# Next tokens of a fused attention and FFN kernel: transposes on TensorE, or in 32x32 squares on VectorE with DMAs that place the squares

## The chip, the cores and the metric

The kernel runs on one core of one Trainium2 chip. The metric is the device time of one execution in microseconds (us); lower is better. A core has five engines that run programs of their own: TensorE (PE in the profile), VectorE (DVE), ScalarE (ACT), GpSimd (POOL) and SyncE (SP), which here issues nearly all DMAs.

## The reference

Eight sequences of 512 tokens with 512 features, in fp32. Each is normalised, goes through a linear attention and through a gated FFN with Hadamard transforms, and the two results are multiplied and added to the input:

```python
xn = _layernorm(x, axis=-1)
q, k, v = xn @ Wq.T + bq, xn @ Wk.T + bk, xn @ Wv.T + bv          # 512 -> 512
kv_sum = cumsum((elu(k) + 1) * v, axis=tokens)
s = ((elu(q) + 1) * kv_sum * SCALE) @ Wo.T + bo
h = fwht(xn * SU_ug) / 64                                          # Hadamard over 512
h = silu(h @ W_gate.T * (wg * 64)) * (h @ W_up.T * (wu * 64))      # 512 -> 2048
g = silu((fwht(h * SU_dp) / 64) @ W_down.T * (Wscale_dp * 64))     # 2048 -> 512
out = x + s * g
```

## The kernel before

*Pairs and factors.* The eight sequences are taken in four pairs `p`, two sequences `s` at a time. All large products are done by a Strassen-like scheme: a 2x2 block product in seven products instead of eight, with sums and differences of blocks before and after. The seven factors of an operand are called `P1, P2, P7, P3, P4, P5, P6` (places 0 to 6). The operand with the tokens is `xo`, a tile of 128 x 7 x 7 x 256: 128 features on the partitions, 7 outer factors, 7 inner factors, 256 tokens. The outer 2x2 blocks are sequence by half of the features: P1 and P2 are the two halves of the first sequence's features, P3 and (for a while) P7 those of the second's; P5, P6, P4 and the final P7 are differences of these. The inner blocks are half of the tokens by tile of 128 features, places 0 to 3; the other three are differences. `group` uses outer factors alone, `block_product` both.

*Getting the tokens.* `load_x` (L105) loads a sequence with tokens on the partitions, `layernorm` (L116) normalises it on VectorE, with one square root on ScalarE. `transposed` (L137) then brings features onto the partitions: for each of four token tiles, four TensorE transposes into one PSUM tile `pt` (L142). For the first sequence of a pair ScalarE copies `pt` into the outer factors P1 and P2 (L146); for the second, ScalarE copies one half (L149) and VectorE forms P5, P6 and P7 with one operand from PSUM (L150 to L152), and at last P4 (L155). At the start of a later pair `inner_tokens` (L157) forms the inner factors P5, P6 and P4 for all seven outer factors. `xo` is allocated anew for each pair in a pool with one buffer.

*A pair.* `attention` makes the key, value and query products (`group`, L306) and the scan over the tokens; `project_out` the output product, kept in DRAM as `d_s`. Then four hidden units `u` follow: in the first pair `gate` and `up` on folded weights, which also make the weights of later pairs and store them in DRAM (`inner_w`, whose sums `s_gate` and `s_up` take the one buffer of the pool `xin`, as `load_x` does for later sequences); in later pairs `hidden_unit` (L647), which calls `block_product` (L467) for seven outer factors in the order P1, P5, P6, P2, P7, P3, P4. After two units `down` does half of the last product, after four the other half, with the gating of the output:

```python
steps += [(p2, 0), (p6, 0), (p2, 1), (p6, 1)]
steps += [(p, g) for p in (p5, p3, p4) for g in range(2)]
```

`token_groups` (L376) runs it: first `p1` and `p7` for two halves `g` of the tokens, then the steps above. Three kinds of PSUM bank are used: `px` (three buffers), `py` (one) and `pz` (two). `p2` multiplies into `py` and VectorE empties it with `output` (L406); so `p2(1)` can start only when the output of `p2(0)` is done. `read` (L402) takes an intermediate sum out of `px` (`sa_dn`, `sb_dn`, `sc_dn`). Each factor `i` has a weight tile, loaded by `get_w` in the order P1, P7, P2, P6, P5, P3, P4: `w_down_0`, `w_down_2`, `w_down_1`, `w_down_6`, `w_down_5`, `w_down_3`, `w_down_4` (the number is the place). The second `down` of a pair also needs the kept sums `d` (twice) and `s` (twice), fetched from DRAM, and the inputs `y` (twice), loaded again, 1 MB each; `gated` applies SiLU on ScalarE (L710), multiplies on POOL (L712), and adds on VectorE (L713).

*What sets the order.* The Python code uses a small agenda (`at`, `advance`) to interleave steps of neighbouring products. After that a scheduler gives each engine its program: it takes instructions by priority (order in the code; `background()` puts a piece 150 places back) as their operands are expected to be ready. The resulting program of each engine is fixed when the kernel is built. An engine carries it out in order, so an instruction that waits for a semaphore holds all that stands behind it on that engine; for SP this is true of the DMAs it issues. A tile in a pool with one buffer can be filled again only when all readers of its last content are done.

Of the kernel before, what the change touches and what calls it, by code (L numbers as in the profile page):

```python
# [8 lines left out]
F32 = mybir.dt.float32  # L9
AF = mybir.ActivationFunctionType  # L10
ALU = mybir.AluOpType
# [6 lines left out]
P1, P2, P7, P3, P4, P5, P6 = range(7)  # L18
# [3 lines left out]
def kernel(  # L22
# [27 lines left out]
    nc = tc.nc  # L50
    P = 128
    B, L, D = x.shape
    FF = wup_t.shape[1]
    KD = D // P
# [4 lines left out]
    H = L // 2  # L59
# [4 lines left out]
    xop = ctx.enter_context(tc.tile_pool(name="xop", bufs=1))  # L64
    hop = ctx.enter_context(tc.tile_pool(name="hop", bufs=2))
    wpool = ctx.enter_context(tc.tile_pool(name="wpool", bufs=4))
    xin = ctx.enter_context(tc.tile_pool(name="xin", bufs=1))
# [4 lines left out]
    dram = ctx.enter_context(tc.tile_pool(name="dram", bufs=1, space=DRAM))  # L72

    @contextmanager
    def background(behind=150):

        at = tc.cur_priority
        tc.cur_priority = at + behind
        yield
        tc.cur_priority = at  # L80
# [4 lines left out]
    at = 0  # L85
# [19 lines left out]
    def load_x(b, t=None, parts=1):  # L105
        if t is None:
            t = xin.tile([P, 3, 7, P], F32, tag="x", name=f"x_{b}")
            t = t.rearrange("p c s e -> p (c s e)")[:, : NT * D].rearrange("p (n d) -> p n d", n=NT)
        n = NT // parts
        for i in range(0, NT, n):  # L110
            nc.sync.dma_start(
                t[:, i : i + n], x[b, i * P : (i + n) * P, :].rearrange("(n p) d -> p n d", p=P)
            )
        return t

    def layernorm(b, xt, parts=1):  # L116
        n = NT // parts
        for i in range(0, NT, n):
            mv = small.tile([P, n, 2], F32, tag="mv", name=f"mv_{b}_{i}")
            for t in range(n):  # L120
                st = small.tile([P, 6], F32, tag="st", name=f"st_{b}_{i}_{t}")
                nc.vector.bn_stats(st, xt[:, i + t, :])
                nc.vector.bn_aggr(mv[:, t, :], st)
            rstd = small.tile([P, n], F32, tag="rstd", name=f"rstd_{b}_{i}")
            nc.vector.tensor_scalar(rstd, mv[:, :, 1], EPS, None, ALU.add)
            nc.scalar.activation(rstd, rstd, AF.Sqrt)
            nc.vector.reciprocal(rstd, rstd)
            for t in range(n):
                nc.vector.tensor_scalar(
                    xt[:, i + t, :], xt[:, i + t, :], mv[:, t, 0:1], rstd[:, t : t + 1],  # L130
                    ALU.subtract, ALU.mult,
                )

    def transposed(b, xt, xo):  # L137
        s = b % 2
        for t in range(NT):
            pt = ps.tile([P, KD, P], F32, tag="t", name=f"pt_{b}_{t}")  # L140
            for c in range(KD):
                nc.tensor.transpose(pt[:, c, :], xt[:, t, c * P : (c + 1) * P], ident)  # L142
            q = 2 * (t // 2)
            o = xo[:, :, q : q + 2, t % 2 * P : t % 2 * P + P]
            if s == 0:
                nc.scalar.copy(o[:, P1 : P2 + 1], pt.rearrange("p (h j) t -> p h j t", h=2))  # L146
            else:
                b12, b22 = pt[:, 0:2], pt[:, 2:4]
                nc.scalar.copy(o[:, P3], b22)  # L149
                nc.vector.tensor_tensor(o[:, P5], b12, o[:, P1], ALU.subtract)  # L150
                nc.vector.tensor_tensor(o[:, P6], b22, o[:, P5], ALU.subtract)
                nc.vector.tensor_tensor(o[:, P7], o[:, P3], b12, ALU.subtract)  # L152
        if s == 1:
            o = xo[:, :, 0:4]
            nc.vector.tensor_tensor(o[:, P4], o[:, P2], o[:, P6], ALU.subtract)  # L155

    def inner_tokens(xo):  # L157

        nc.vector.tensor_tensor(xo[:, :, P5], xo[:, :, P7], xo[:, :, P1], ALU.subtract)
        nc.vector.tensor_tensor(xo[:, :, P6], xo[:, :, P3], xo[:, :, P5], ALU.subtract)  # L160
        nc.vector.tensor_tensor(xo[:, :, P4], xo[:, :, P2], xo[:, :, P6], ALU.subtract)

    def inner_t3(xo, factors):
        for i in factors:
            nc.vector.tensor_tensor(xo[:, i, P7], xo[:, i, P3], xo[:, i, P7], ALU.subtract)
# [17 lines left out]
    kept = {}  # L183
# [102 lines left out]
    def at(place, fn):  # L286
        agenda.append((now[0] + place, now[1], fn))
        now[1] += 1
# [10 lines left out]
    def drain():  # L299
        advance(max([0] + [e[0] + 1 - now[0] for e in agenda]))  # L300
# [572 lines left out]
    def get_w(m, g):  # L873
# [15 lines left out]
    xs = [  # L889
        load_x(b, hop.tile([P, 2, 7, D], F32, tag="h", name=f"x_{b}")[:, 0, :NT], parts=2)  # L890
        for b in range(2)
    ]
# [5 lines left out]
    for i in range(7):  # L898
        dst = had if i % 2 == 0 else had2
        s = src.rearrange("p (a t h) -> p a t h", t=2, h=1 << i)  # L900
        d = dst.rearrange("p (a t h) -> p a t h", t=2, h=1 << i)
# [3 lines left out]
    xo = xop.tile([P, 7, 7, H], F32, tag="xo", name="xo_0")  # L905
# [29 lines left out]
    for p in range(B // 2):  # L935
        if p:
            with background():
                inner_tokens(xo)
        co = attention(p, xo, get_w)
        if p:  # L940
            inner_t3(xo, (P1, P5, P6, P2, P7))
            at(9, lambda: inner_t3(xo, (P3, P4)))
        more = p + 1 < B // 2
        hos = []

        def next_x():
            xs = [load_x(2 * p + 2), load_x(2 * p + 3)]
            for s in range(2):
                layernorm(2 * p + 2 + s, xs[s])
            return xs  # L950

        for u in range(NU):
            if p == 0:
                gs = [gate(p, u, xo, get_w)]
                gs.append(gate(p, u + NU, xo, get_w))
                if u == 0:
                    project_out(p, co, get_w)
                ho = hop.tile([P, 2, 7, L], F32, tag="h", name=f"ho_{p}_{u}")
                for m in range(2):
                    up(p, u + m * NU, gs[m], xo, ho[:, m], get_w)  # L960
            else:
                ho = hop.tile([P, 2, 7, L], F32, tag="h", name=f"ho_{p}_{u}")
                hidden_unit(p, u, xo, ho, get_w, u % 2 == 1)
                if u == 0:
                    project_out(p, co, get_w)
            hos.append(ho)
            if more and u == (2 if p else 3):
                xs = next_x()
            if u == 1:
                down(p, 0, hos, get_w)  # L970
                hos = []
        if more:
            xo = xop.tile([P, 7, 7, H], F32, tag="xo", name=f"xo_{p + 1}")
            for s in range(2):
                transposed(2 * p + 2 + s, xs[s], xo)
        ds, ss = [], []
        for s in range(2):
            ds.append(fetch(f"d_{p}_{s}"))
            ss.append(fetch(f"s_{p}_{s}"))
        ys = [load_y(p, s) for s in range(2)]  # L980
        down(p, 1, hos, get_w, ds, ss, ys)
        drain()
# [50 lines left out]
```

## Time and profile before

| what | value |
|---|---|
| time, median of three runs | 1605.21 us (1602.78 to 1605.37) |
| the profiled execution | 1606.13 us, span 1604.3 us from first to last instruction |
| PE busy | 1550.9 us, 97% |
| VectorE, ScalarE, POOL busy | 949.2, 425.1, 504.9 us |
| granted TensorE clock, mean | 0.992 |
| DMA | 254.29 MB, 47.9% of 16 engines' span on SP's queue |
| TensorE transposes (L142) | 128 |

The page of the profile gives busy times per engine, a chain of work that ended last (followed back from the last instruction to what released each step), and groups of instructions by source line with their mean duration and the idle time before them. A timeline lists one engine's instructions in order of time: start, duration, engine and line, operation, output and inputs, shape, count, and in brackets the idle time before it and who ended it. In this trace every fp32 matmul is recorded as two instructions: a `down` step of 8 matmuls appears as x16. Durations of neighbouring matmuls overlap, so what a stretch of PE costs is read from the starts.

### The profile page before, as it was taken

How to read it: one execution, taken by the hardware profiler on the slowest of the kernel's cores; microseconds unless marked ns; L12 is line 12 of the kernel's file. 1: busy time of each engine (PE TensorE's matmuls, PEld its weight loads, DVE VectorE, ACT ScalarE, POOL GpSimd, SP SyncE). 2: the span in 40 equal slices, each digit the busy share in tenths (PEclk: the TensorE clock that was granted, in tenths of full speed). 3: DMA queues.
4: the chain of work that ended last, by engine and by line, in shares of the span. 5: the costliest groups of instructions: out<-in, count | busy, mean ns of one | idle time of the engine just before them, and what ended most of it. 6: DMA issues, size and time to landing. Idle time of an engine off the chain costs nothing.

```text
span 1604.3 us, 15681 instructions
## 1 busy us (share of the span) xinstructions
PE 1550.9 (97%) x5936; PEld 1117.1 (70%) x5936; DVE 949.2 (59%) x1335; ACT 425.1 (26%) x679; POOL 504.9 (31%) x286
## 2 busy tenths in 40 slices
PE   6979989999999999999999999999999999999998
PEld 3335435854485478888886478888887468888887
DVE  6869666268565574715675475634675466542673
ACT  3333322132324431111222531111221441111211
POOL 4531342103322235302622236201622137120731
PEclk9999999999999999999999999999999999999999
DMA  8234559397763244335574232535474224525472
GB/s 266 80 111 135 180 148 300 84 280 215 250 218 129 69 138 145 131 107 189 178 255 144 90 107 102 193 91 188 158 265 157 69 93 137 176 83 190 141 261 84
DMA packets 147723, 254.29 MB, mean 159 GB/s; under 512 B 7232, under 2 KB 109120, under 8 KB 143552
## 3 DMA queue, kind: packets, MB, share of 16 engines
q1 hardware_dynamic: 147360, 253.00, 47.9%
q8 instruction: 47, 0.77, 0.2%
q10 hardware_dynamic: 288, 0.30, 0.1%
q14 instruction: 28, 0.23, 0.0%
HBM read 183.53 MB, written 69.73 MB: 158 GB/s over the span
## 4 chain that ended last, share of the span: by engine, by line
PE 73%; DVE 12%; DMA 5%; issue 4%; POOL 3%; ACT 2%; SPq 1%; POOLq 0%; DVEq 0%; ACTq 0%
PE px_gu L475 18%; PE pz_gu L475 9%; PE px_dn L391 8%; PE py_gu L475 5%; PE pz_dn L391 4%; PE px_o L391 3%; PE px_v L316 3%; PE px_k L316 3%; PE px_q L316 3%; PE py_dn L391 2%; DMA x<-in_x_dram 2%; POOL s L712 2%; PE pz_o L391 2%; PE pz_q L316 2%; PE pz_k L316 1%
## 5 line engine op out<-in xcount | busy, mean ns | idle before, releaser
L475 PE MATMUL px_gu<-xo,w_gu 128*128 128x256 f32 x1344 | 320.6, 380 | 0.0
L475 PEld LDWEIGHTS px_gu<-xo,w_gu 128*128 128x128 f32 x1344 | 254.7, 190 | 39.9 <-issue 3.6
L391 PE MATMUL px_dn<-w_down,ho 128*128 128x256 f32 x1024 | 230.1, 379 | 2.2 <-DVE sb_dn L402 1.7
L391 PEld LDWEIGHTS px_dn<-w_down,ho 128*128 128x128 f32 x1024 | 193.6, 190 | 31.4 <-DVE sb_dn L402 2.7
L475 PE MATMUL pz_gu<-xo,w_gu 128*128 128x256 f32 x672 | 173.1, 380 | 0.0
L675 POOL TENSOR_TENSOR u<-u,v 128x1024 f32<-128x1024 f32 x24 | 56.1, 2360 | 354.2 <-DVE u L513 354.2
L475 PEld LDWEIGHTS pz_gu<-xo,w_gu 128*128 128x128 f32 x672 | 127.0, 190 | 19.1 <-DVE a L517 0.9
L391 PE MATMUL pz_dn<-w_down,ho 128*128 128x256 f32 x512 | 116.6, 380 | 1.9 <-POOL ho L172 1.9
L391 PEld LDWEIGHTS pz_dn<-w_down,ho 128*128 128x128 f32 x512 | 96.4, 190 | 17.6 <-POOL ho L172 2.7
L712 POOL TENSOR_TENSOR s<-s,d 128x512 f32<-128x512 f32 x30 | 43.0, 1435 | 166.2 <-ACT d L710 166.2
L475 PE MATMUL py_gu<-xo,w_gu 128*128 128x256 f32 x336 | 86.2, 379 | 0.0
L563 POOL TENSOR_TENSOR v<-v,k 128x1024 f32<-128x1024 f32 x16 | 39.8, 2486 | 138.5 <-ACT v L538 110.3
L637 POOL TENSOR_TENSOR ho<-g,u 128x512 f32<-128x512 f32 x8 | 17.8, 2224 | 186.0 <-DVE u L332 186.0
L475 PEld LDWEIGHTS py_gu<-xo,w_gu 128*128 128x128 f32 x336 | 63.9, 190 | 8.7
L316 PE MATMUL px_k<-xo,w_k 128*128 128x512 f32 x128 | 63.0, 616 | 3.7 <-ACT sa_k L328 3.4
L316 PE MATMUL px_up<-xo,w_up 128*128 128x512 f32 x128 | 60.4, 600 | 4.0 <-DVE w_up L178 4.0
L679 POOL TENSOR_TENSOR v<-v,r 128x1024 f32<-128x1024 f32 x24 | 56.2, 2364 | 25.6 <-DVE r L513 25.6
L316 PE MATMUL px_v<-xo,w_v 128*128 128x512 f32 x128 | 60.2, 593 | 3.5 <-ACT sc_v L328 3.5
L316 PE MATMUL px_q<-xo,w_q 128*128 128x512 f32 x128 | 60.2, 593 | 0.0
L316 PE MATMUL px_gate<-xo,w_gate 128*128 128x512 f32 x128 | 59.6, 593 | 0.0
L565 DVE TENSOR_TENSOR_SCAN k<-ones,v 128x512 f32<-128x512 f32 x32 | 39.4, 1271 | 33.5 <-POOL v L563 33.5
L391 PE MATMUL py_dn<-w_down,ho 128*128 128x256 f32 x256 | 58.0, 379 | 0.0
(241 smaller groups left out, 2469.0 us busy)
## 6 DMA issues: line engine op xcount, KB each, us to landing
w_gu<-d_gu SPq DMA_DIRECT2D x84, 896.0 KB, 4.5
w_down<-d_down SPq DMA_DIRECT2D x56, 512.0 KB, 3.6
d_s<-o SPq DMA_DIRECT2D x8, 1024.0 KB, 4.4
d_d<-dn SPq DMA_DIRECT2D x8, 1024.0 KB, 7.5
d<-d_d SPq DMA_DIRECT2D x8, 1024.0 KB, 6.2
s<-d_s SPq DMA_DIRECT2D x8, 1024.0 KB, 7.3
y<-in_x_dram SPq DMA_DIRECT2D x8, 1024.0 KB, 8.4
out_dram<-y SPq DMA_DIRECT2D x16, 512.0 KB, 3.1
```

The costliest lines, as they stand in the source:

```text
L316: nc.tensor.matmul(p.rearrange("p a t -> p (a t)") if len(r.shape) == 2 else p, ws[k][:, i, :], r, start=(first and k == 0), stop=(k == n ...
L391: nc.tensor.matmul(p[:, c], t[:, (2 * g + c) * P : (2 * g + c + 1) * P], ws[i](k), start=(first and k == 0 and c == 0), stop=(k == n - 1), ...
L475: nc.tensor.matmul(p[:, lane], w[:, lane, i, :], x[:, i, :], start=(first and lane == 0), stop=True, skip_group_check=True,)
L563: nc.gpsimd.tensor_tensor(v[:, h], v[:, h], k[:, h], ALU.mult)
L565: nc.vector.tensor_tensor_scan(k[:, h, s], ones.to_broadcast([P, L]), v[:, h, s], 0.0, ALU.mult, ALU.add)
L637: nc.gpsimd.tensor_tensor(ho[:, P1], g[:, 0, 0], r[:, 0, 0], ALU.mult)
L675: nc.gpsimd.tensor_tensor(r[:, m], ru1[:, m], rv[:, m], ALU.add)
L679: nc.gpsimd.tensor_tensor(rv[:, m], rv[:, m], rr[:, m], ALU.add)
L712: (nc.vector if last else nc.gpsimd).tensor_tensor(r, r, d, ALU.mult)
```

## The change

The first pair is as before. For later pairs three new steps replace `next_x` and the TensorE transposes:

- `normalized(b)` loads and normalises a sequence and stores the result in DRAM as `d_x`. It is called after hidden units 0 and 1 of the pair before, in the background, instead of after unit 2 or 3.
- `squares(b)` loads the stored sequence back into a tile `z` in the pool `xin` with 16 DMAs. Each moves 32x32 squares: for a block `j` of 32 features within a feature tile `c`, the 32 tokens of each of the 16 token blocks go to the partitions `32 j` to `32 j + 31`. Every run is 32 features, 128 bytes.
- `turned(place, z, h, xo)` transposes the squares in place on VectorE, 32x32 at a time, straight into the outer factor `place` of `xo`: two instructions of 128x512 per factor.

`next_tokens` puts them together after the last hidden unit and ahead of the second `down`, with the differences P5, P6, P7 and P4 on VectorE from SBUF. `xo` is no longer allocated for each pair: one tile, made for the first pair, is written again for all.

```diff
+    def normalized(b):
+
+        xt = load_x(b)
+        layernorm(b, xt)
+        d = dram.tile([L, D], F32, tag=f"d_x_{b}", name=f"d_x_{b}")
+        nc.sync.dma_start(d.rearrange("(n p) d -> p n d", p=P), xt)
+        kept[f"x_{b}"] = d
+
+    def squares(b):
+
+
+        z = xin.tile([P, 3, 7, P], F32, tag="x", name=f"z_{b}")
+        z = z.rearrange("p c s e -> p (c s e)")[:, : KD * L].rearrange("p (c i f) -> p c i f", c=KD, f=32)
+        d = kept[f"x_{b}"].rearrange("(i t) (c j f) -> j t c i f", t=32, j=4, f=32)
+        for j in range(4):
+            for c in range(KD):
+                nc.sync.dma_start(z[32 * j : 32 * j + 32, c], d[j, :, c])
+        return z
+
+    def turned(place, z, h, xo):
+
+        for j in range(2):
+            nc.vector.transpose(
+                xo[:, place, j : j + 3 : 2, :], z[:, 2 * h + j].rearrange("p i f -> p (i f)")
+            )
+
+    def next_tokens(b, xo):
+
+        o = xo[:, :, 0:4]
+        z = squares(b)
+        turned(P1, z, 0, xo)
+        turned(P2, z, 1, xo)
+        z = squares(b + 1)
+        turned(P7, z, 0, xo)
+        nc.vector.tensor_tensor(o[:, P5], o[:, P7], o[:, P1], ALU.subtract)
+
+        def rest():
+            turned(P3, z, 1, xo)
+            nc.vector.tensor_tensor(o[:, P6], o[:, P3], o[:, P5], ALU.subtract)
+            nc.vector.tensor_tensor(o[:, P7], o[:, P3], o[:, P7], ALU.subtract)
+
+        def last():
+            nc.vector.tensor_tensor(o[:, P4], o[:, P2], o[:, P6], ALU.subtract)
+
+        at(5, rest)
+        at(10, last)
...
-        def next_x():
-            xs = [load_x(2 * p + 2), load_x(2 * p + 3)]
-            for s in range(2):
-                layernorm(2 * p + 2 + s, xs[s])
-            return xs
...
-            if more and u == (2 if p else 3):
-                xs = next_x()
+            if more and u < 2:
+                with background():
+                    normalized(2 * p + 2 + u)
             if u == 1:
                 down(p, 0, hos, get_w)
                 hos = []
         if more:
-            xo = xop.tile([P, 7, 7, H], F32, tag="xo", name=f"xo_{p + 1}")
-            for s in range(2):
-                transposed(2 * p + 2 + s, xs[s], xo)
+            next_tokens(2 * p + 2, xo)
```

## Prediction

> **What bounds the kernel now.** I read the page first, then the stretches of 25 us, then each engine's timeline around the three places where one pair of sequences hands over to the next. I call these seams: seam 1 lies at about 430 to 498 us, seam 2 at 800 to 869, seam 3 at 1169 to 1238. A seam holds the second `down` of a pair, the transposes of the next pair's tokens, and the next pair's first key product.
>
> ```profile
> PE 1550.9 (97%) x5936; PEld 1117.1 (70%) x5936; DVE 949.2 (59%) x1335; ACT 425.1 (26%) x679; POOL 504.9 (31%) x286
> PE 73%; DVE 12%; DMA 5%; issue 4%; POOL 3%; ACT 2%; SPq 1%; POOLq 0%; DVEq 0%; ACTq 0%
> ```
>
> TensorE (PE) is busy 97% of the span and carries 73% of the chain that ended last. From 300 us on, nearly every stretch of 25 us is full; what is missing lies at the seams. So only two things move the time: work taken off PE, and waits of PE. The PE timeline of seam 2 and then of seam 1 shows both:
>
> ```profile
> 807.88 1.04 PE L142 MATMUL pt<-ident,x 128*128 128x128 f32 x8
> 808.75 1.89 PE L391 MATMUL px_dn<-w_down,ho 128*128 128x256 f32 x8
> ...
> 826.49 3.62 PE L391 MATMUL py_dn<-w_down,ho 128*128 128x256 f32 x16
> ...
> 835.63 3.62 PE L391 MATMUL py_dn<-w_down,ho 128*128 128x256 f32 x16
> ...
> 868.93 1.98 PE L316 MATMUL px_k<-xo,w_k 128*128 128x512 f32 x4 [0.94 <-ACT sa_k L328]
> ```
> ```profile
> 451.62 1.03 PE L391 MATMUL px_dn<-w_down,ho 128*128 128x256 f32 x4
> 453.22 1.99 PE L391 MATMUL pz_dn<-w_down,ho 128*128 128x256 f32 x8 [0.57 <-POOL ho L172]
> 455.05 3.62 PE L391 MATMUL py_dn<-w_down,ho 128*128 128x256 f32 x16
> ...
> 497.77 2.93 PE L316 MATMUL px_k<-xo,w_k 128*128 128x512 f32 x3 [2.28 <-ACT sa_k L328]
> ```
>
> Eight transposes hold PE for 808.75 - 807.88 = 0.87 us. The first `py_dn` of a seam is `p2(0)` of `down`, the first use of weight tile `w_down_1`; the second is `p2(1)`. The bracket is PE's idle time before the line. All idle time in seam 1 is 0.73 + 0.57 + 0.26 + 2.28 = 3.8 us.
>
> The queue of SyncE (SP) in seam 1 shows what stands before that weight tile:
>
> ```profile
> 434.98 12.74 SPq L203 DMA_DIRECT2D w_down<-d_down  x2
> 450.62 0.38 SPq L738 DMA_DIRECT2D y<-in_x_dram  x1
> 451.12 0.44 SPq L111 DMA_DIRECT2D x<-in_x_dram  x1
> 451.60 0.51 SPq L738 DMA_DIRECT2D y<-in_x_dram  x1
> ```
>
> `w_down_1` and `w_down_6` are the x2 at 434.98: ahead of both `y`, and on time. A wait in this queue holds everything behind it.
>
> **What the Trainium skill says.** "VectorE: DVE Perf Modes", The three transpose paths: VectorE transposes 32x32 blocks only, and takes 311 ns for 128x128 in bf16. No VectorE transpose is in this trace. "DMA: Bandwidth & Descriptors", Anatomy of one DMA: a semaphore wait happens on the issuing sequencer, before dispatch. The trace agrees: the x2 above occupy SP for 12.74 us, mostly waiting. Same page, Queues, rings and completion order: each DMA engine consumes descriptors in ring order. The trace agrees: the `x` issued at 451.12 landed 7.46 us later, behind the `y` of 450.62. Same page, Why small descriptors are slow (HBM only): a packet costs its size over 32 bytes, plus about 3 cycles; by that 128 bytes take 7/19 of the time of 512.
>
> **The change, part by part.** The order of instructions in the two built programs is fixed, so I place each piece by it.
>
> (1) *Transposes off PE.* 96 of 128 go: 12 groups of eight, 12 x 0.87 = 10.4 us less for PE. ScalarE's copies (L146, L149) and VectorE's L150 to L152 go too, from engines with idle time.
>
> (2) *Normalisation moved.* The VectorE work is the same. For the first hand-over it moves to about 232 and 286 us, where VectorE idled 6.65 and 10.65 us; one pass takes about 4 x 0.6 + 4 x 0.48 + 0.7 = 5.0. It adds a table switch of 1.28 us each way on ScalarE, and `x` and its store take the one buffer (`xin`) that the weight sums `s_gate` also use. Price 0 to 4 us, I take 1.5. For later pairs the built order puts the normalisation into the previous seam's `down`, about where it was. There the second load waits for the first's store (4 to 5 us), since `xin` has one buffer. The six stores of 1 MB lie under matmuls: nothing, unless a seam's queue is full.
>
> (3) *Square loads.* Each sequence needs 16 DMAs on SP's queue, each of 512 runs of 128 bytes. Issue: four loads of `w_v` take 1.91 us at 37.44, so 0.48 each, 7.7 us for a set. Transfer: the trace's packet records give 27 ns for 512 bytes, 18 for 256, so about 13 for 128: 512 packets per engine and set, 6.7 us. No row shows 128 bytes; bounds 10 ns, and 27 if small ones gain nothing (13.8 us). I take 13.
>
> (4) *VectorE transposes.* Eight of 128x512 fp32 per seam. A 128x512 operation runs here at one per 0.60 us, and the skill's 311 ns for 128 columns fits one element a cycle plus a start: I take 0.62, bounds 0.35 and 1.2. Four differences of 1024 columns cost 1.18 each (L155: 1.22 alone), and `inner_tokens` 3 x 2.0 as before (L159 to L161). A block from the second set's first transpose to `inner_tokens` is 4 x 0.62 + 4.7 + 5.9 = 13.1 us, and the built order leaves it in one piece: the sums that free PE's banks stand behind it.
>
> *Seam 1.* The built order is, on SP: first set, `s`, second set, `d`, `s`, `y`, `y`, then `w_down_1`. On VectorE: both early `sa_dn` reads, four transposes of the first set, then the block. PE without its two first groups and the 0.73 ends its early products at 449.7; POOL's `ho` steps, 1.8 us sooner, release `pz_dn`, and PE is ready for `p2(0)` at 453.1. The second read ends at 450.5, the four transposes at 453.0, and only then is the buffer free for the second set. SP issues it until 460.7, then `d`, `s`, `y`, `y` (4 MB) until 462.2, then `w_down_1`. Two MB took 7.96 us from the issue at 450.62 to landing (451.12 + 7.46 = 458.58), about 2 x 2.85 + 2.2. So 4 MB and half a MB of weights from 460.7: 4 x 2.8 + 1.3 + 2.2 = 14.7, landing at 475. The block ends at 475 as well. `p2(0)` starts at 475.0 instead of 455.05: +19.9. After it two groups (1.74), the 0.26 and some 1.1 of the final 2.28 go. Sum **+16.8**.
>
> *Seams 2 and 3.* The first set comes during attention and is turned inside the last hidden unit; the second is issued from 796.6 (13 of its DMAs after a weight's wait that ends at 802.0) to 808.6 and lands by 811, so it is covered, at 27 ns also. `w_down_1`, behind the last `y` (818.8), lands at about 825, when PE (two groups less) wants it at 824.75. But the block starts at 822.1, after `sa_dn`, and ends at 835.5; the sum that empties `py` comes behind it, at 836.1. PE finishes `p6(0)` at 831.7 and waits 4.6 us for `p2(1)`, which starts at 836.3 where it was 835.63: +0.7, all four groups saved being spent. Following VectorE on, behind the later second `x`, the key product waits 1.9 us instead of 0.94, the pause of 0.87 shrinks to 0.3: +0.4. Seam 2 **+1.1**; seam 3 had only 1.08 of such idle time left: +0.7 + 1.1 = **+1.8**.
>
> *Sum:* 1.5 + 16.8 + 1.1 + 1.8 = +21.2. The profiled execution was 1606.1 (span 1604.3 and 1.8 around it), so 1627.3; it stands 0.9 above the median of 1605.2, so a median of 1626.
>
> **The rivals.** *(a) PE alone decides, and it gets faster.* The added waits lie under matmuls: the block on VectorE, 13.1 us, is hidden, and `w_down_1` comes by 453. Then 10.4 and about 2 us of idle time go: 1593. For it: PE is the 97% engine, VectorE idles 41%. Against it: the built order, with `w_down_1` behind two sets and 4 MB. It decides as soon as the waits together stay under 12 us. *(b) Small packets are dear.* HBM reads of 128 bytes cost three times the line, 40 ns: a set takes 20.5 us. Seam 1 then turns the first set at 454.7, has the second at 475 and `w_down_1` at 489 (+14), and in seams 2 and 3 the weights come at about 835 (+6.5 each): 1626 + 27 = 1653; at 54 ns about 1682. For it: no such packet is in the trace. Against it: packets of 512 and 256 bytes lie on one line. *(c) The weights don't queue behind the 4 MB.* If transfers share the engines, `w_down_1` lands 3.6 us after 462.2, and the block, ending at 475, binds `p2(1)` instead of 482: 6.6 less, 1620.
>
> **How the numbers follow.** My forecast 0.61, (b) 0.20, (c) 0.11, (a) 0.08. The forecast's own bounds: transposes at 0.35 or 1.2 move each seam by -1.1 or +2.3, packets of 10 or 27 ns move seam 1 by -1.5 or +7, the first stage by -1.5 or +2.5. Downwards these give about 1615, upwards 1643. The range 1612 to 1646 holds the forecast, (c) and a third of (b); it leaves out (a) and the dearer packets, some 0.2. About 0.2% (3.2 us) is what a measurement of this kernel can tell from no change: faster 0.06, same 0.02 (both from (a), when only part of the waits is hidden), slower 0.92.
>
> **What would show it.** Right: no `pt` after the first pair; in seam 1 a PE wait of about 22 us ahead of the first `py_dn`, ended by the DMA of `w_down`; in seams 2 and 3 a wait of about 4.6 us ahead of the second `py_dn`, ended by VectorE's sum; VectorE transposes of about 0.62 us; a set landing about 10 us after its first issue. Wrong: seams without such waits, transposes or packets outside the bounds, or a new PE wait in the first 300 us of more than 4 us.

## The result and the profile after

| | before | changed kernel |
|---|---|---|
| time, median | 1605.01 us (6 runs, 1602.78 to 1605.37) | 1627.26 us (6 runs, 1621.41 to 1629.31) |
| ratio | | 1.0130, 95% interval 1.0111 to 1.0149 |
| the profiled execution | 1606.13 us, span 1604.3 | 1621.41 us, span 1619.6 |
| TensorE transposes | 128 | 32 |

The change costs 22 us; the forecast was 1626.0. The profiled execution is the shortest of the six runs, 5.9 us below their median; f4 below is a second profile of the same kernel (1625.7 us).

The busy times and the clock row on the page of the changed kernel:

```profile
PE 1539.2 (95%) x5840; PEld 1108.1 (68%) x5840; DVE 963.0 (59%) x1332; ACT 414.6 (26%) x655; POOL 503.0 (31%) x286
...
PE   6989989999949999999999999999999999999998
PEld 3336435844536468888877468888878458888887
...
PEclk9999999999979999999999999999999999999999
```

PE works 11.7 us less than before (1550.9), and yet the span is 15.3 us longer. The twelfth of the 40 slices has a hole: PE at 4 tenths, its clock at 7. The list of PE's waits (us in total, times, longest) names it:

```profile
PE py_dn L439 <- DMA w_down<-d_down: 30.3, 3, 22.8
...
PE py_dn L439 <- DVE d L454: 0.6, 1, 0.6
```

Three waits of `p2(0)` for its weight tile, one in each seam; in the list of before there is no such line. Seam 1 on PE's timeline of the changed kernel, then seam 2:

```profile
447.95 1.99 PE L439 MATMUL pz_dn<-w_down,ho 128*128 128x256 f32 x8 [1.35 <-POOL ho L220]
472.78 5.34 PE L439 MATMUL py_dn<-w_down,ho 128*128 128x256 f32 x16 [22.84 <-DMA w_down<-d_down]
...
843.02 3.72 PE L439 MATMUL py_dn<-w_down,ho 128*128 128x256 f32 x16 [3.57 <-DMA w_down<-d_down]
846.58 3.62 PE L439 MATMUL px_dn<-w_down,ho 128*128 128x256 f32 x16
850.77 3.72 PE L439 MATMUL py_dn<-w_down,ho 128*128 128x256 f32 x16 [0.58 <-DVE d L454]
```

SP's queue in seam 1 and in seam 2, where the wait is made:

```profile
426.26 9.09 SPq L151 DMA_DIRECT2D z<-d_x  x16
435.39 0.49 SPq L642 DMA_DIRECT2D s<-d_s  x1
449.76 8.27 SPq L151 DMA_DIRECT2D z<-d_x  x16
458.13 0.43 SPq L642 DMA_DIRECT2D d<-d_d  x1
458.60 0.43 SPq L642 DMA_DIRECT2D s<-d_s  x1
459.14 1.35 SPq L786 DMA_DIRECT2D y<-in_x_dram  x2
460.58 4.38 SPq L251 DMA_DIRECT2D w_down<-d_down  x4
...
826.32 0.43 SPq L642 DMA_DIRECT2D s<-d_s  x1
826.85 0.38 SPq L642 DMA_DIRECT2D d<-d_d  x1
827.32 0.38 SPq L642 DMA_DIRECT2D s<-d_s  x1
831.22 3.01 SPq L786 DMA_DIRECT2D y<-in_x_dram  x2
834.32 5.49 SPq L251 DMA_DIRECT2D w_down<-d_down  x4
```

In seam 1 SP stands still from 435.9 to 449.8: the second set has no buffer. Then come 16 issues, 4 MB, and only then `w_down_1`, which PE has wanted since 449.9. What ends SP's wait is seen on VectorE's timeline of the same stretch: the last transposes of the first set.

```profile
447.25 2.48 DVE L157 STREAM_TRANSPOSE xo<-z 128x512 f32<-128x512 f32 x4
458.31 1.31 DVE L157 STREAM_TRANSPOSE xo<-z 128x512 f32<-128x512 f32 x2 [8.58 <-DMA z<-d_x]
...
469.77 2.03 DVE L209 TENSOR_TENSOR xo<-xo 128x1792 f32<-128x1792 f32 x1
```

2.48 for four is 0.62 us each. The block runs from 458.31 to 471.80 in one piece. It ends only 1 us before `p2(0)` starts, but the trace's records of landings tell what ends the wait: `d`, `s`, `y` and `y`, issued from 458.1 on, land in the order of their issue at 463.3, 465.9, 468.9 and 471.4, and `w_down_1` behind them at 472.74, 0.04 us before `p2(0)`.

*Where the time went.* Both kernels have the same 5808 matmuls besides the transposes, so the start of the n-th one can be compared. The median of the difference (changed minus before) in a quiet stretch after each seam, and its steps:

| stretch of before | difference, first profile | step | difference, f4 | step | forecast step |
|---|---|---|---|---|---|
| 300 to 425 us | -3.42 | first stage -3.4 | -0.40 | -0.4 | +1.5 |
| 525 to 790 | +15.01 | seam 1 +18.4 | +18.46 | +18.9 | +16.8 |
| 895 to 1150 | +15.52 | seam 2 +0.5 | +20.48 | +2.0 | +1.1 |
| 1265 to 1570 | +15.31 | seam 3 -0.2 | +19.60 | -0.9 | +1.8 |

Seam 1 is nearly all of it. (f4's first stage is 3.0 us slower than the first profile's; its section below treats why.)

### The profile page after: what moved, and what is told of

It reads as the page before. It is cut to its first block, busy times and chain, and to the rows that moved or that the text cites. A ratio compares the mean times of both kernels' runs of the same rounds, so it can differ in the third digit from the quotient of the medians.

```text
span 1619.6 us, 15596 instructions
## 1 busy us (share of the span) xinstructions
PE 1539.2 (95%) x5840; PEld 1108.1 (68%) x5840; DVE 963.0 (59%) x1332; ACT 414.6 (26%) x655; POOL 503.0 (31%) x286
## 4 chain that ended last, share of the span: by engine, by line
PE 81%; DVE 8%; issue 3%; POOL 3%; DMA 3%; ACT 1%; SPq 1%; POOLq 0%; DVEq 0%; ACTq 0%
PE px_gu L523 18%; PE px_dn L439 10%; PE pz_gu L523 9%; PE pz_dn L439 5%; PE py_gu L523 4%; PE px_o L439 3%; PE py_dn L439 3%; PE px_up L364 3%; PE px_v L364 3%; PE px_k L364 3%; PE px_q L364 3%; PE px_gate L364 2%; PE pz_o L439 2%; PE pz_up L364 1%; PE pz_k L364 1%
## 5 line engine op out<-in xcount | busy, mean ns | idle before, releaser
L523 PEld LDWEIGHTS pz_gu<-xo,w_gu 128*128 128x128 f32 x672 | 127.2, 190 | 18.4 <-DVE a L565 0.9
L760 POOL TENSOR_TENSOR s<-s,d 128x512 f32<-128x512 f32 x30 | 38.5, 1285 | 192.3 <-ACT d L758 192.3
L439 PE MATMUL py_dn<-w_down,ho 128*128 128x256 f32 x256 | 61.5, 396 | 30.9 <-DMA w_down<-d_down 30.3
L439 PEld LDWEIGHTS py_dn<-w_down,ho 128*128 128x128 f32 x256 | 50.7, 199 | 39.8 <-DMA w_down<-d_down 31.5
L758 ACT ACTIVATE d<-d 128x512 f32<-128x512 f32 x32 | 20.2, 630 | 185.8 <-DVE d L454 151.0
```

What stands on the lines that cost most here:

```text
L439: nc.tensor.matmul(p[:, c], t[:, (2 * g + c) * P : (2 * g + c + 1) * P], ws[i](k), start=(first and k == 0 and c == 0), stop=(k == n - 1), ...
L523: nc.tensor.matmul(p[:, lane], w[:, lane, i, :], x[:, i, :], start=(first and lane == 0), stop=True, skip_group_check=True,)
L758: nc.scalar.activation(d, d, AF.Silu)
L760: (nc.vector if last else nc.gpsimd).tensor_tensor(r, r, d, ALU.mult)
```

## The experiments

All are read with the same comparison of starts. The steps of each, from its profile, and its times:

| kernel | first stage | seam 1 | seam 2 | seam 3 | median, us | ratio to before (95%) |
|---|---|---|---|---|---|---|
| e1, weights first | -0.4 | +7.7 | +1.9 | -1.5 | 1614.6 | 1.0067 (1.0044 to 1.0089) |
| e2, more weights first | -0.6 | +8.0 | +1.6 | +0.2 | 1615.1 | 1.0066 (1.0044 to 1.0087) |
| e3, long runs | +3.5 | +7.9 | +4.7 | +2.2 | 1622.6 | 1.0107 (1.0082 to 1.0132) |
| e4, normalise early alone | -1.6 | +2.0 | +2.4 | -0.5 | 1608.4 | 1.0026 (1.0012 to 1.0040) |
| f3, own buffer | -0.2 | +8.3 | +2.2 | +1.2 | 1616.3 | 1.0076 (1.0052 to 1.0100) |
| f1, old first seam | +0.1 | (+24.1) | +1.7 | +0.5 | 1632.3 | 1.0170 (1.0146 to 1.0194) |
| f2, f1 with inner differences held | -1.9 | (+26.6) | 0.0 | -2.7 | 1629.6 | 1.0154 (1.0133 to 1.0175) |
| g1, f1 normalised later | -0.8 | (+7.0) | +16.3 | +16.8 | 1645.5 | 1.0253 (1.0226 to 1.0279) |
| g2, g1 with inner differences held | -1.8 | (+3.8) | +19.3 | +20.4 | 1647.9 | 1.0257 (1.0236 to 1.0277) |
| g3, all repairs | -1.8 | -2.6 | +0.4 | -3.0 | 1600.6 | 0.9972 (0.9957 to 0.9987) |
| h1, before with inner differences held | -2.6 | +0.6 | +0.1 | -0.1 | 1606.1 | 1.0007 (0.9999 to 1.0016) |

The kernel before ran beside each batch, with medians of 1604.3 to 1605.4. Where an edit is shown it is against the changed kernel.

**e1: the weights ahead of the second set.** `ask(n)` requests weight tiles until n are under way.

```diff
         turned(P2, z, 1, xo)
+        ask(4 if b == 2 else 3)
         z = squares(b + 1)
```

> Theory (the weight tile w_down_1 lands late because it is queued behind the second set and 4 MB): with w_down_1 and w_down_6 asked for ahead of the second set (in later seams w_down_1 alone), the wait of 22.8 us ahead of the first py_dn in seam 1 goes; what is late next is w_down_5, now the one behind the 4 MB: it lands at about 471.5, PE wants it at about 464, so some 8 us come back at px_dn. In seams 2 and 3 the waits of 3.6 and 3.9 us on w_down_1 go and at most 1 us stays. In all 18 to 22 us less than the changed kernel: 1605 to 1609. Rival (VectorE's block, which ended at 471.8 just ahead of the first py_dn, is what holds PE): seam 1 gains less than 2 us, the whole less than 6: above 1621. Rival (PE's clock after a pause makes most of the loss): a shorter pause gains more than its length, below 1600.

Measured: 1614.6, 12.7 us less than the changed kernel, between the theory and its first rival; the clock rival (below 1600) falls. The theory's mechanism is there in seam 1 and its sizes are not. The wait moved to `w_down_5`, but it is 12.4 us and not 8; in seams 2 and 3 PE waits for VectorE where it had waited for the weights. PE's timeline of e1:

```profile
479.21 15.51 PE L440 MATMUL px_dn<-w_down,ho 128*128 128x256 f32 x64 [12.39 <-DMA w_down<-d_down]
...
836.06 3.72 PE L440 MATMUL py_dn<-w_down,ho 128*128 128x256 f32 x16 [0.78 <-DVE d L455]
839.62 7.07 PE L440 MATMUL px_dn<-w_down,ho 128*128 128x256 f32 x32
849.95 15.77 PE L440 MATMUL px_dn<-w_down,ho 128*128 128x256 f32 x64 [3.26 <-DVE sb_dn L451]
```

In seam 2 the waits for weights and sums are 0.78 + 3.26 = 4.0 us, against 3.57 + 0.58 + 0.80 = 5.0 in the changed kernel, and in seam 3 0.78 + 3.10 = 3.9 against 3.92. So there the late weights covered a wait for VectorE's sums that is nearly as long. About 2.0 of the 3.26 us come from two of VectorE's differences ahead of that sum, which POOL held up (last section). The rival that VectorE's block alone held PE in seam 1 falls: the wait in front of `p2(0)` is gone. (In e1's built order the first sums also stand ahead of the block; that the block didn't end the wait in the changed kernel is shown by the landing above.)

**e2: `w_down_5` and `w_down_3` ahead of the 4 MB too.** As e1, with

```diff
         z = squares(b + 1)
+        if b == 2:
+            ask(6)
```

> As the one before, and in seam 1 w_down_5 and w_down_3 are also asked for ahead of the 4 MB, behind the second set. Theory (queue order alone): w_down_5 lands at about 463.5, as PE wants it; left is some 3 us, where the third products wait for VectorE's sum behind its block (about 474 instead of 471). Time 1598 to 1604, faster than the kernel before. Rival (bandwidth: 5 MB more or less have to come through in this stretch whatever their order): what is saved at the weights comes back at d and y, 1608 or more.

Measured: 1615.1. The wait for weights in seam 1 is gone and another has its place, 8.95 us at the next step that needs VectorE:

```profile
482.45 9.74 PE L442 MATMUL px_dn<-w_down,ho 128*128 128x256 f32 x32 [8.95 <-DVE sc_dn L453]
```

The theory had put that at 3 us: it took the block to end at 474. In the built program the first four sums stand ahead of the block, so it began at 467.2, when PE had made them possible, and ended at 481.8. The time agrees with the bandwidth rival (1608 or more), but not its cause: the release is a sum on VectorE, not `d` or `y`.

**e3: the same loads in long runs.** The sets come in runs of 2048 bytes, with the squares not in their places.

```diff
-        d = kept[f"x_{b}"].rearrange("(i t) (c j f) -> j t c i f", t=32, j=4, f=32)
+        d = kept[f"x_{b}"].rearrange("(j c t) f -> j c t f", c=KD, t=32)
...
-                nc.sync.dma_start(z[32 * j : 32 * j + 32, c], d[j, :, c])
+                nc.sync.dma_start(z[32 * j : 32 * j + 32, c].rearrange("p i f -> p (i f)"), d[j, c])
```

> The sets are loaded with the same 16 DMAs of 64 KB each, but in runs of 2048 bytes instead of 128, so the squares are not in their places and later pairs compute on shuffled tokens; the work of all engines is the same. Theory (a set takes as long as SP needs to issue 16 DMAs, 8.3 us, and the packets of 128 bytes, 6.7 us an engine, lie under that): at most 1 us in seam 1 and nothing in the others, 1625 to 1628. Rival (the small packets cost engine time that the weights wait for: 6.7 against 2.7 us a set): 4 us in seam 1 and some in the others, 1622 or less.

Measured: 1622.6, between the two and nearer to the rival (1622 or less). The lines of seam 1 (PE, then SP) tell it apart:

```profile
468.99 5.44 PE L439 MATMUL py_dn<-w_down,ho 128*128 128x256 f32 x16 [12.15 <-DMA w_down<-d_down]
```
```profile
447.26 7.28 SPq L151 DMA_DIRECT2D z<-d_x  x16
```

From the first issue of the second set to the start of `p2(0)` it takes 468.99 - 447.26 = 21.7 us; in the changed kernel 472.78 - 449.76 = 23.0. The chain is shorter by 1.3 us, of which 1.0 is SP's issue (7.28 against 8.27). The wait is shorter by 10.7 for another reason: in this built program the first set's transposes stand ahead of the `sa_dn` reads, and PE came to the seam 6.9 us later, so SP began the second set 9.6 us before PE wanted `w_down_1`, instead of together with it. So the wait is a chain of about 22 us less the lead that it has. In e3's profile two other things take back part of this gain. The first stage is at half clock for 27.3 us (13.7 in the first profile), and in seams 2 and 3 the waits for `w_down` are longer, 5.8 and 5.6 us, where the theory had no change: in seam 2 SP issues the second `y` only at 835.0, after a wait of 4.7 us for VectorE's `ho` (2.2 in the changed kernel); the built order has put that `ho` behind part of the block. The weights stand behind this `y`.

**e4: the normalisation moved alone,** with TensorE's transposes kept. The stored sequences are loaded again in the old layout; the edit is against the kernel before (the helpers `normalized` and `again` are left out).

```diff
-            xs = [load_x(2 * p + 2), load_x(2 * p + 3)]
-            for s in range(2):
-                layernorm(2 * p + 2 + s, xs[s])
-            return xs
+            return [again(2 * p + 2), again(2 * p + 3)]
...
+            if more and u < 2:
+                with background():
+                    normalized(2 * p + 2 + u)
             if more and u == (2 if p else 3):
                 xs = next_x()
```

> Only the normalisation is moved: sequences are normalised after hidden units 0 and 1 of the pair before and stored, loaded again in the old place in the old layout, and transposed on TensorE as before. Forecast's term: +1.5 us in the first stage, so 1606.5. Rival (its work lies in idle time of VectorE; the 3.4 us by which the changed kernel was ahead at 430 us in its profile come from when TensorE's clock was at half, not from the change): within 1.5 us of the kernel before, either sign. Rival (the move itself gives 3.4 us): 1601.5.

Measured: 1608.4, 0.26% (0.12 to 0.40) above before, so the move with its reload is not free. But its steps lie in seams 1 and 2 (+2.0, +2.4), where PE's transposes wait for the reload (5.3 us in four waits in its list), and not in the first stage (-1.6). The forecast's term, 1.5 us in the first stage, finds no support; and that the move gives 3.4 us is refuted.

**f3: a buffer of its own for the second set of seam 1.**

```diff
+        if b == 3:
+            z = t8.tile([P, KD, 16, 32], F32, tag="t", name=f"z_{b}")
+        else:
...
```

> The changed kernel with one thing different: in seam 1 the second set has a buffer of its own (one of t8's), so its loads need not wait until the first set is transposed at 449.7 us in the trace of the changed kernel. Theory (the wait is a chain: first set's transposes, second set's 16 issues, 4 MB, w_down_1): the chain starts some 10 us earlier, the wait ahead of the first py_dn falls from 22.8 to 8 to 13 us, 1614 to 1619. Rival (w_down_1's own buffer or y's buffers come free late in any case): 18 us or more of wait are left, 1622 or more.

Measured: 1616.3, 10.9 us less than the changed kernel. SP issues all 32 loads in one row from 426.5 to 445.7, and PE's wait in seam 1 is as the theory had it:

```profile
465.05 6.16 PE L442 MATMUL py_dn<-w_down,ho 128*128 128x256 f32 x16 [9.78 <-DMA w_down<-d_down]
```

`w_down_1` landed at 465.01. With e1 this shows the chain from two sides: its start moved forward (f3), or the weight taken out from behind its links (e1).

**f4: the changed kernel again.**

> The changed kernel once more, for a second profile. Theory (its executions at 1621.5 and at 1628 us differ in how many windows of 3.4 us TensorE spends at half clock after its pauses, each costing up to 1.7 us): the same waits as in the first profile within 0.5 us, and the difference in span explained by span times the difference in mean granted clock. Rival (DMA times differ from execution to execution): the wait of 22.8 us moves by 2 us or more.

Measured: 1625.7 us, span 1623.9. The waits for `w_down` are 30.1 us in three, the longest 22.7, against 30.3 and 22.8. So transfers are alike, and what differs is the clock. Stretches around seam 1 of the first profile of the changed kernel (from and to; length; busy us of PE, PEld, DVE, ACT and POOL; then PE's clock, the DMA share and GB/s) show how it goes:

```profile
450.00:460.00 10.00, 0.00 (x0) 0.00 (x0) 1.66 (x3) 0.00 (x0) 0.00 (x0) 0.61 0.75 116
460.00:470.00 10.00, 0.00 (x0) 0.00 (x0) 9.86 (x9) 0.00 (x0) 0.00 (x0) 0.50 1.00 380
...
475.00:480.00 5.00, 5.00 (x22) 4.28 (x21) 0.69 (x1) 1.10 (x2) 0.41 (x1) 0.89 0.67 263
480.00:485.00 5.00, 5.00 (x25) 4.41 (x24) 4.11 (x10) 0.82 (x1) 0.86 (x1) 1.00 0.01 3
```

While PE waits, its clock goes to half, and stays there for some microseconds after work has come back: the first `py_dn` takes 5.34 us instead of 3.62. The trace's clock records show that stretches at half last 3.41 us or a multiple of it (but for the last one, which the end of the program cuts), and that within a trace all begin on one grid of this step. "TensorE: Matmul & The Clock Gate", Part 1: The HAM clock gate, of the Trainium skill tells of a free-running window of 3413 ns, and with that the trace agrees. The same section has the clock halved after a whole idle window, and there the traces differ: a part of one is enough. The fourteen traces were divided into these windows (from 30 us on), and PE's idle time between matmul records was added up in each. Of 6338 windows at full clock, all 101 with 2.02 us or more of idle time are followed by half clock, and none of the others, with up to 2.01 us, is. Of 159 windows at half clock, the 87 that full clock follows have at most 0.59 us of idle time; the rest have 0.74 or more, but for one with 0.49.

In the first stage, seam 1, seam 2 and seam 3 the changed kernel spent 13.7, 23.9, 0 and 3.4 us at half in the first profile, and 17.1, 23.9, 6.8 and 3.4 in the second: 10.2 us more, worth up to 5.1 at half speed, beside a span that is 4.3 longer. The theory's arithmetic holds roughly as well: 1619.6 x 0.014 = 22.7 us lost against 1623.9 x 0.017 = 27.6.

**f1 and f2: the first seam old, the others new; and the inner differences held back.** I wanted the share of each seam from f1. In seam 1 it doesn't give it: the old transposes write into the same `xo`, and stand in the built order ahead of the last `up` products of the first pair, which so read tokens of the next pair; that part of the computation is changed in f1, f2, g1 and g2, and their seam 1 (in brackets in the table) is not the old one. The sequences of seam 1 were also loaded a unit too early in f1 and f2. Only seams 2 and 3 are read from these four. f2's edit against f1 puts the inner differences behind the first head:

```diff
+        late = small.tile([P, 1], F32, tag="late", name="late")
+        nc.vector.tensor_scalar(late, co[:, 0, 0, 0:1], 0.0, 1.0, ALU.mult, ALU.add)
+        nc.vector.scalar_tensor_tensor(
+            xo[:, :, P5], xo[:, :, P7], late, xo[:, :, P1], ALU.mult, ALU.subtract
+        )
...
-        if p:
-            with background():
-                inner_tokens(xo)
         co = attention(p, xo, get_w)
         if p:
+            inner_tokens(xo, co)
```

`late` is always 1, but can be computed only when a part of the first head's result is there.

> The first seam as before the change (normalised after unit 2 into xin, TensorE transposes); seams 2 and 3 with squares, and w_down_1 asked for ahead of the second set. Theory (nearly all of the loss is seam 1's; in seams 2 and 3 the waits on w_down_1 were covering waits for VectorE's sums behind its block, so asking earlier gives nothing there): seams 2 and 3 together between -1 and +1.5 us, 1604 to 1606.5, no difference from the kernel before. Rival (with the weights in time, the four transposes saved in each of two seams show): 1605 - 7 = 1598. Rival (something of the change outside seam 1 costs as well): above 1610.

> As the one before, and the three inner differences (5.9 us of VectorE's block), which only the hidden units need, are tied to the first head's result, so that they run inside attention. Theory (the block ahead of the sums is what binds in seams 2 and 3): the waits of 0.8 us at the second py_dn and 3.2 us at the px_dn after it shrink to 1.5 together, so each of the two seams ends 2 to 4 us earlier than before the change: 1597 to 1601. Rival (PE waits for something else behind that, such as y or d from DRAM): within 1 us of the one before. Rival (the differences inside attention hold up its scan): above 1607.

Measured: the times fit none of the theories, since seam 1 alone cost 24 and 27 us. In seams 2 and 3 together f1 has +2.1 us and f2 -2.7, so holding the differences is worth 4.9 there, of the 2 to 4 each that the theory gave. In f1 PE waits 6.5 us in two for `sb_dn`, one in each of these seams:

```profile
866.77 15.57 PE L440 MATMUL px_dn<-w_down,ho 128*128 128x256 f32 x64 [3.25 <-DVE sb_dn L451]
```

In f2 these waits are gone; the 0.78 at the second `py_dn` stays. The 4.9 us hold some clock as well: each of f1's two waits is followed by 3.4 us at half clock, and f2 has no such stretch there.

**g1 and g2: the same two with the loads where they should be.** In these the later sequences are also held until units 1 and 2 are done, so that their loads don't come ahead in seam 1.

> The first seam as before the change (normalised after unit 3 of the first pair, TensorE transposes); seams 2 and 3 with squares, their sequences normalised after units 1 and 2 and not earlier, and w_down_1 asked for ahead of the second set. Theory (nearly all of the loss is seam 1's; in seams 2 and 3 the waits on w_down_1 cover waits for VectorE's sums behind its block, so asking earlier gives nothing there): seams 2 and 3 together between -1 and +2.5 us, 1604 to 1607.5, no difference from the kernel before. Rival (with the weights in time, the four transposes saved in each of two seams show): 1605 - 7 = 1598. Rival (something of the change outside seam 1 costs as well): above 1610.

> As the one before, and the three inner differences (5.9 us of VectorE's block), which only the hidden units need, are tied to the first head's result, so that they run inside attention. Theory (the block ahead of the sums is what binds in seams 2 and 3): the waits of 0.8 us at the second py_dn and 3.2 us at the px_dn after it shrink to 1.5 together, so seams 2 and 3 together are 3 to 6 us shorter than in the one before: 1599 to 1603. Rival (PE waits for something else behind that, such as y or d from DRAM): within 1 us of the one before. Rival (the differences inside attention hold up its scan): above 1607.

Measured: 1645.5 and 1647.9, all theories wrong. The cause is visible and is the chain of seam 1 again, now in seams 2 and 3. The first set comes so late that its transposes release the buffer only at 832.1; SP then issues the second set in one row, then `s`, `d`, `s`, `y`, `y`, then the weights. Seam 2 of g1 on SP, then PE:

```profile
832.12 8.29 SPq L154 DMA_DIRECT2D z<-d_x  x16
...
844.46 6.34 SPq L255 DMA_DIRECT2D w_down<-d_down  x4
```
```profile
858.70 16.63 PE L443 MATMUL px_dn<-w_down,ho 128*128 128x256 f32 x68 [11.10 <-DMA w_down<-d_down]
```

From 832.12 to 858.70 are 26.6 us, with 5 MB instead of 4 and the second weight tile instead of the first. Since this wait is the longer one, holding the inner differences gains nothing (g2). The chain is not all of the +16.3 us: just ahead of the seam PE waits another 4.5 us for VectorE's sum `a`, which the built order has put behind the later normalisation (780.5 to 788.5 us), and 13.7 us of this seam are at half clock. Seam 3 is alike.

**g3: all repairs, squares in all seams.** f3's buffer, f2's held differences, and the weights early: in seam 1 behind both sets and ahead of the 4 MB, else ahead of the second set.

```diff
+        if b > 2:
+            ask(3)
         z = squares(b + 1)
+        if b == 2:
+            ask(4)
```

> Squares in all three seams, with the repairs together: in seam 1 a buffer of its own for the second set and w_down_1 and w_down_6 asked for behind both sets but ahead of the 4 MB, in the others w_down_1 ahead of the second set, and the inner differences held back. Theory: in seam 1 the first sums come some 3 us late behind the shorter block and w_down_5 is about on time, against four groups of transposes and about 2 us of idle time saved: -2 to +2 us; seams 2 and 3 -3 together; 1600 to 1605. Rival (w_down_5 stays late behind the 4 MB, as in e1): 1608 to 1612.

Measured: 1600.6 us in 8 runs, ratio 0.9972 (0.9957 to 0.9987): 4.8 us (0.3%) less than the kernel before, which ran beside it, a small gain but clear of noise by its interval. Seam 1 gives -2.6, a little more than expected, and the others -2.6 together; the -1.8 of the first stage is no gain of the repairs, since h1, which changes nothing there, has -2.6. What is left of the waits for weights and sums in seams 1 and 2 (seam 3 has 0.78 as well):

```profile
466.90 14.05 PE L450 MATMUL px_dn<-w_down,ho 128*128 128x256 f32 x64 [0.52 <-DMA w_down<-d_down]
...
824.29 3.72 PE L450 MATMUL py_dn<-w_down,ho 128*128 128x256 f32 x16 [0.78 <-DVE d L465]
```

**h1: a control, the kernel before with only the inner differences held.** The edit of f2 on the kernel before.

> A control: the kernel before the change, TensorE transposes and all, with only the three inner differences held back into attention, as in the version with all repairs. Theory (that version's gain of about 4.5 us comes from the transposes taken off TensorE, once nothing waits for them): here nothing is gained, since the waits for VectorE in its seams are below 1 us: 1603.5 to 1607. Rival (the gain was that of the held differences, and the transposes are worth nothing): 1601 or less.

Measured: ratio 1.0007 (0.9999 to 1.0016), no gain. So what g3 wins does not come from the held differences alone. It comes with the rest of g3, and that this is the transposes off TensorE, once nothing waits for what replaces them, is inferred: the early weights can't have won it, since PE's list of waits in the kernel before has none for `w_down`, and e4 shows no gain from the early normalisation.

## Why the prediction was right, point by point

*The total* was right: 1626.0 forecast, 1627.3 measured. The sum of steps was +21.2 against +15.3 in the first profile and +19.6 in the second. Part of this agreement is luck, since the errors cancel: against f4 the first stage was forecast 1.9 us too high and seam 3 2.7, seam 1 2.1 too low and seam 2 0.9.

*(1) Transposes off PE.* Forecast -10.4 us; PE's busy time fell by 11.7. Right, and none of it is seen in the time.

*(2) Normalisation moved.* Forecast +1.5 in the first stage. f4, whose stretches at half clock there are nearly those of before, has -0.4; over f4, e1, e2 and f3 it is -0.2 to -0.6; e3, at half clock for 10 us more, has +3.5. The term was too high. The 3.4 us by which the first profile was ahead are probably clock for the most part: before has a stretch of 6.8 us at half clock from 105 us, where PE was at work.

*(3) Square loads.* Issue 8.27 us a set, 0.52 each (forecast 7.7, 0.48). A packet of 128 bytes takes 13.0 ns in the trace, 49152 of them: the value taken, from the line through 512 and 256 bytes. The Trainium skill's "DMA: Bandwidth & Descriptors", Why small descriptors are slow (HBM only), would have given an estimate of 7/19 of the 27.6 ns of 512 bytes, 10.2 ns; the measurement lies above it. e3 shows that the small packets hardly lengthen the chain, which rival (b) needed.

*(4) VectorE transposes.* 0.62 us each, as estimated; the block 13.5 us against 13.1.

*Seam 1.* The mechanism is the forecast's, link by link: the second set issued when the first is turned (forecast 453.0; 449.8 in the profile, which entered the seam 3.4 ahead: 453.2), a wait of 22.84 us (about 22), ended by the DMA of `w_down`. The size was +18.4 and +18.9 against +16.8. Counted from the entry, `p2(0)` is 17.7 + 3.4 = 21.1 us later, not 19.9: `w_down_1` went out at 464.0 in the forecast's time, not at 462.2, since the issues take longer. A term was missing on both sides: the restart at half clock costs 1.7 us (5.34 - 3.62), and before had such a stretch too, at its `px_k` after 2.28 us of idleness (3.58 instead of 1.88).

*Seams 2 and 3.* Here a step failed: "`w_down_1`, behind the last `y` (818.8), lands at about 825". The tile went out about when forecast, 0.5 us after the last `y`, but landed 8.7 us later instead of 6.2. In the profile the DMAs `s`, `d`, `s` were issued in one row at 826.3 to 827.3, because the second set's loads had held them up, and were not through when `y`, `y` came: 5 MB and half a MB from 826.3, at the forecast's own 2.8 us a MB, are 5.5 x 2.8 + 2.2 = 17.6 us, so 843.9; PE got it at 843.0. The forecast's 6.2 us name the `y` alone there, though in seam 1 it had counted all four. That the sum still came out is no accident, but not foresight either: the wait on the weights (3.57) lay over the wait for VectorE's block (4.6 forecast). e1 took the first away and the second stood there with 0.78 + 3.26 = 4.0 us. The place was not quite that of the forecast: 0.58 at the second `py_dn` in the changed kernel, and in e1 mostly at the `px_dn` after it, since its built order lets the first sums in between pieces of the block.

*The rivals.* (a) fell at once: PE's 10 us are hidden behind 30 us of waits. It is what remains when the waits are taken away: g3 has 5 us of it. (b) is refuted by the 13.0 ns. (c), that weights don't queue behind the 4 MB, is refuted by the landing of `w_down_1`, 12.2 us after its issue at 460.6 where (c) had 3.6, and 1.3 us behind the last `y`.

*What stays open.* g3 is 8.8 us ahead of before at 838 us, in seam 2, and only 4.1 at the values' products (921.6). A `px_k` at half clock is part of it. So is a wait of 1.73 us for ScalarE's `sc_v`, which has come into each later attention (8.7 us in four waits instead of 3.5 in one). It comes with the held differences: h1 has it and before has not, and likewise f2 and not f1, g2 and not g1. In g3 the chain can be followed: VectorE's held differences at 910.2 and 913.0 push its sum `k` back to 918.1, ScalarE waits 5.72 us for that `k`, and its read of `sc_v` stands behind. A better place for the differences was not tried. It is also open which of g3's repairs could be left out, since no version with only two of them was run with squares in all seams. The share of seam 1 alone, with the old transposes there and all else new, was not measured, since in f1 and g1 the old transposes overwrite tokens that are still in use.

## What to carry to other kernels

When work is moved off the busy engine through DRAM, cost the chain that feeds the next stage, not the engine: which transfer waits for which buffer on the in-order queue, and which weight stands behind it. Count all bytes that were issued in the few microseconds before the transfer that matters, not only the last ones; what a stalled queue lets out comes in one row. And where a wait is taken away, look at once for the one that lay under it: here the buffer or the order of weights alone gave back about half, and of the versions that were run only the one with all repairs (with the block of VectorE work not needed yet held back too) made the moved transposes pay.

## What the runs showed that I had not expected

- TensorE's clock goes with differences of several us between runs of the same program: the changed kernel's six runs have mean clocks of 0.982 to 0.986 and spans of 1627.5 to 1619.6. Where a pause falls on the grid of 3.41 us matters as much as its length: 2.28 us in before lay with 2.10 us in one window and was followed by half clock. A pause of 3.57 us in the first profile of the changed kernel (seam 2) was cut into 1.87 and 1.70 and was not, and 3.92 us (seam 3) filled a window and was.
- On VectorE, a 32x32 transpose of fp32 tiles of 128x512 from SBUF to SBUF takes 0.62 us in a row of them (one alone is recorded with 0.67 to 0.71); sums of the same size are spaced 0.60 us.
- POOL holds VectorE up. VectorE's differences of 128x1024 and 128x1792 within `xo` took 2.29 us instead of 1.22 and 2.98 instead of 2.02 in places (e1, at 837.1 and 845.1). Both times an operation of POOL was under way (836.8 to 838.3 and 843.9 to 846.2), and VectorE's ended 1.1 and 1.9 us after POOL's was done. The fourteen traces have 257 of these differences. All 56 that took at least 1.57 or 2.50 us had begun while POOL was at work and ended 1.08 or 1.88 us after it; the 191 that began with POOL idle took at most 1.23 and 2.03.
